# Block results stored by token instead of by block in a two-layer metaformer on one core

## The chip, the cores and the metric

The kernel runs on one core of a Trainium2 chip. The metric is the device time of one execution in microseconds (us), as the median over runs; a profiled execution gives the trace from which durations are read. The core has five engines with a queue each: TensorE (PE, with its weight loads PEld), VectorE (DVE), ScalarE (ACT), GpSimd (POOL) and SyncE (SP). Each runs its own queue in order, and they wait for each other by semaphores. DMAs are issued from SP, ACT and POOL; those with an index per row ("indirect") are issued from POOL here.

## The reference

Everything is float32. x has four images of 384 channels and 32 x 32 tokens. Two layers follow each other, each a mixer and a feed-forward part, with residuals:

```python
x = x + _L0_conv_ref(_ln_c(x), ...)      # attention, 8 heads of 48, relative positions in q, k and v, then proj
t = _to_tokens(x)
t = t + _L0_ffn_ref(_ln_t(t), ...)       # weights are Kronecker products, gelu between
x = _from_tokens(t, x)
x = x + _L1_conv_ref(_ln_c(x), ...)      # sum of depthwise convolutions, at most 7x7
t = _to_tokens(x)
t = t + _L1_ffn_ref(_ln_t(t), ...)       # 4 experts 384 -> 1536 -> 384, each token gated to its best two
x = _from_tokens(t, x)
```

`_ln_c` and `_ln_t` normalise each token over its 384 channels. The expert part takes a softmax over four scores, keeps the two largest, divides them by their sum, and adds the two experts' results with these weights.

## The kernel before

P is 128, C is 384, KC = 3 chunks of channels, N = 1024 tokens an image, B = 4 images, BLK = 128. Sizes in DMA rows are rows of C float32, 1536 bytes. The kernel has three phases.

**qkv_phase** (0 to about 237 us). Eight tiles of 512 tokens. `load(t)` brings a tile of x, three loads bring `wq` (384 x 1152). `token_stats` transposes a tile with `ident` (L75), takes mean and variance on DVE (L77, L78) and 1/deviation (L84, L85); `to_partitions` turns it into a row for all partitions (s_dg L103, all_ps L105). `center` subtracts from each column of the weights its mean, by matmuls with `one` (L116) and DVE (L118), once, ahead of the tiles. Then come six q and k products (qk_ps L163, qk_sb L167, stored to qk_d by POOL) and four v products (v_ps L174), which ACT writes into `va`, 64 wide per head of which 48 are filled; the other 16 have to be zero. `va` is cleared as a whole by POOL at the start (L135), ahead of `ident`'s second step on POOL. From tile 2 to 5 POOL also writes zeros over the whole of `xs_d` (L190, eight DMAs of 3 MB), the padding of the dispatched rows.

**attention_phase** (to about 1663 us) is not touched.

**rest_phase** (to the end). Per image: `front` (proj L903/L906 and the Kronecker feed-forward, L921 to L952), `normalise`, `image` (a padded picture `img`), `convolve`, gates, dispatch. `convolve` runs 49 taps on DVE, one instruction per chunk of channels and tap (L993, 128 x 1024). For image 0 DVE does chunk 0 and the first `own` = 4 rows of chunk 1; the other rows of chunk 1 and chunk 2 are done on PE at the same time by `taps_by_matmul`: four parts (two of 16 rows, two of 14), 196 matmuls each with diagonal weights (L1037), sums by L1047/L1048, added into the image on DVE (L1051). Three steps of this generator are taken per tap of DVE.

`gates` yields for each token its two experts (`mask`) and weights (`gate`), and the normalised token rows. `scatter` computes for each token a slot in its experts' lists (`slot_positions`; `rank` is the place in the list) and POOL writes the rows to `xs_d` by index (L1103), 16 writes of 128 rows an image; `block_list` then makes the list of blocks. A *block* is 128 slots of one expert: 67 blocks in four groups of COUNTS = 13, 16, 16 and 22; the groups follow the images as they are dispatched. For block k, POOL fetches the rows `xg` (L1147) one block ahead and the weights `w` in two halves by index (L1166), three halves ahead; PE transposes xg (xT_ps L1160); then come twelve steps of a first product (e_ps L1198), Gelu on ACT (L1201) and a second product (y_ps L1176), two steps later. DVE adds the bias (yo L1179) and SP stores 128 rows to `y_d`, in the order of blocks (L1181).

`combine(bs)` turns results into the output. `result_rows` computes on DVE, from `rank` and the group's `pieces` (where each expert's list begins in `y_d`), the two rows of `y_d` that belong to each token; POOL gathers them by index (L1237, 16 of 128 rows an image); ACT and DVE weigh and add (L1249, L1250), PE transposes (L1226), DVE adds the residual (L1227), SP stores (L1228). Images 0 to 2 are combined from block `NOT_LAST` = 6 of the last group on, beside the blocks; image 3 after the last block.

**Order.** A scheduler orders each engine's queue by the order of the program's steps and by when operands are free; instructions passed to `keep_in_program_order` stay as written. The program's order is made by generators: within the blocks `more` keeps a small budget of DVE and PE time, and takes steps from `todo` (= `others`: front, normalise and convolve of images 1 to 3) while it is not spent. Inside `others`, each tap of image b also advances `side`, the dispatch of image b-1, by one step (from the third tap on), and `later`, the front of image b+1 (from the thirteenth). `first` is image 0's convolution.

Of the kernel before, what the change touches and what calls it, by code (L numbers as in the profile page):

```python
# [11 lines left out]
F32 = mybir.dt.float32  # L12
AF = mybir.ActivationFunctionType
ALU = mybir.AluOpType
# [4 lines left out]
P = 128  # L19
# [28 lines left out]
CAP = B * N  # L48

# [16 lines left out]
def token_stats(nc, pools, ident, x, eps, rows=None, step=4):  # L66
# [5 lines left out]
    for j in range(nj):  # L72
# [6 lines left out]
        if rows is not None:  # L79
            nc.scalar.copy(rows[j], ps[:, :C])  # L80
# [40 lines left out]
def qkv_phase(tc, cst, x, w_qkv, qk_d, v_d, xs_d):  # L121
# [6 lines left out]
    with ExitStack() as es:  # L128
# [6 lines left out]
        nc.gpsimd.memset(va, 0.0)  # L135
        zero = wp.tile([P, 1, C], F32, name="zero")
# [10 lines left out]
        for k in range(KC):  # L147
            nc.sync.dma_start(wq[:, k, :], w_qkv[k * P : (k + 1) * P, :])
        stats = result(token_stats(nc, (work, psum, "st"), ident, xts[0], cst["eps6"]))
        center(nc, psum, "st", one, wq)  # L150
        for t in range(NT // TOK):
# [8 lines left out]
            for m in range(2 * KC):  # L160
                ps = psmm.tile([P, TOK], F32, tag="mm", name="qk_ps")
# [7 lines left out]
            if t + 1 < NT // TOK:  # L169
                stats = result(token_stats(nc, (work, psum, "st"), ident, xts[t + 1], cst["eps6"]))  # L170
            for j in range(TOK // P):
# [511 lines left out]
def slot_positions(nc, pools, cst, image, count, total):  # L683


    small, psum = pools
# [12 lines left out]
    rank, pos = image["rank"], new(shape, "pos")  # L699
# [15 lines left out]
    for i, pick in enumerate(chosen(nc, new, mask)):  # L715
        for src, dst in ((pos, fpos), (top, image["gate"])):
            nc.vector.tensor_tensor(prod, pick, src, ALU.mult)
            nc.vector.tensor_reduce(dst[:, :, i : i + 1], prod, AX.X, ALU.add)
    nc.vector.tensor_copy(image["pos"], fpos)
# [14 lines left out]


def result_rows(nc, small, image, pieces):


    shape = list(image["mask"].shape)

    def new(shape, name):
        return small.tile(shape, F32, tag=f"p_{name}", name=f"p_{name}", bufs=1)

    pos, part, step = new(shape, "pos"), new(shape, "prod"), new([P, 1, NEXP], "step")
    nc.vector.tensor_tensor(pos, image["rank"], bcast(pieces[0][1].unsqueeze(1), 1, shape[1]), ALU.add)
    for (_, off0), (lo, off) in zip(pieces, pieces[1:]):
        nc.vector.tensor_tensor(step[:, 0, :], off, off0, ALU.subtract)
        nc.vector.tensor_tensor(part, image["rank"], bcast(lo.unsqueeze(1), 1, shape[1]), ALU.is_ge)
        nc.vector.tensor_tensor(part, part, bcast(step, 1, shape[1]), ALU.mult)
        nc.vector.tensor_tensor(pos, pos, part, ALU.add)  # L750
    row = new([P, shape[1], 2], "fpos")
    for i, pick in enumerate(chosen(nc, new, image["mask"])):
        nc.vector.tensor_tensor(part, pick, pos, ALU.mult)
        nc.vector.tensor_reduce(row[:, :, i : i + 1], part, AX.X, ALU.add)
    nc.vector.tensor_copy(image["pos"], row)


def block_list(nc, small, cst, group, parts, done):
# [24 lines left out]
    for i, (lo, _, falling) in enumerate(parts):  # L783
        turn = slice(None, None, -1) if falling else slice(None)
        begin, off = group["pieces"][i]
        nc.vector.tensor_scalar(begin, lo, float(BLK), None, ALU.mult)
        nc.vector.tensor_scalar(
            off, first[:, i * NEXP : (i + 1) * NEXP, 0][:, turn], float(group["start"]), float(BLK), ALU.add, ALU.mult
        )
        nc.vector.tensor_tensor(off, off, begin, ALU.subtract)  # L790
# [20 lines left out]
    nc.vector.scalar_tensor_tensor(where, over, OUTSIDE, where, ALU.mult, ALU.add)  # L811
    nc.vector.tensor_scalar(where, where, slot[:, 0:1], cst["wrow"][:, 0:1], ALU.add, ALU.add)
# [22 lines left out]
def rest_phase(tc, cst, x, ao_d, ins, xs_d, y_d, x2_d, out):  # L835
# [9 lines left out]
    with ExitStack() as es:  # L845
# [31 lines left out]
        pc = {"before": const("before", [P, P]), "blocks": const("blocks", [P, MAXB]), "wrow": const("wrow", [P, 2])}  # L877
        pc["one"], pc["slot0"] = one, const("slot0", [P, NEXP])
# [105 lines left out]
        def convolve(b, xb, parts):  # L984
# [5 lines left out]
            for dy in range(7):  # L990
                for dx in range(7):
                    for k, y0, y1 in parts:
                        nc.vector.scalar_tensor_tensor(  # L993
                            acc[:, k, y0:y1], img[:, k, dy + y0 : dy + y1, dx : dx + IMG],
                            w7[:, k, dy, dx : dx + 1], acc[:, k, y0:y1], ALU.mult, ALU.add,
                        )

# [15 lines left out]
        def taps_by_matmul(xb, parts):  # L1013
# [15 lines left out]
            for k, y0, ny in parts:  # L1029
# [21 lines left out]
                nc.vector.tensor_tensor(acc, acc, po[:, :n], ALU.add)  # L1051
# [8 lines left out]
        for b, nb in enumerate(COUNTS):  # L1060
# [3 lines left out]
                "rank": new([P, nj, NEXP], f"rank{b}"),  # L1064
# [6 lines left out]
                "pieces": [  # L1071
                    (new([P, NEXP], f"begin{b}{i}"), new([P, NEXP], f"off{b}{i}")) for i in range(1 + (b + 1 == B))
                ],
# [8 lines left out]
        scattered = []  # L1082

        def gates(b):
# [9 lines left out]
            for j, row in enumerate(rows):  # L1094
                nc.scalar.activation(row, row, AF.Identity, bias=shift[:, j, :], scale=rstd[:, j, :])
                im["rows"].append(row)
            yield 0.0, 0.0

        def new_row():
            return hid.tile([P, C], F32, tag="rows", name="rows", bufs=16)  # L1100
# [20 lines left out]
        def scatter(b, pause):  # L1121
            im, g = images[b], groups[b]
            slot_positions(nc, (small, ps_m), pc, im, counts[b], counts[b + 1])
            yield 4.0, 0.5
            for j, rows in enumerate(im["rows"]):
                for s in range(2):
# [14 lines left out]
        def blocks(g, more):  # L1141
# [3 lines left out]
            def fetch(k):  # L1145
                xg = ld.tile([P, C], F32, tag="xg", name="xg")
# [8 lines left out]
            def turn(k):  # L1155
# [6 lines left out]
                xT[k] = t  # L1162
# [11 lines left out]
            def second(k, ff, hs, w, py):  # L1174
                o = WB + ff % FH * C
                nc.tensor.matmul(py, hs, w[:, o : o + C], start=(ff == 0), stop=(ff == NF - 1))  # L1176
                if ff == NF - 1:
                    yo = hid.tile([P, C], F32, tag="yo", name="yo", bufs=2)
                    nc.vector.tensor_tensor(yo, py, w[:, WB + FH * C :], ALU.add)  # L1179
                    n = (g["start"] + k) * BLK  # L1180
                    nc.sync.dma_start(y_d[n : n + BLK, :], yo)  # L1181
# [292 lines left out]
```

## Time and profile before

| | |
|---|---|
| median of 3 runs | 3289.18 us (3285.77 to 3293.74) |
| profiled execution | 3284.5 us, of which the span is 3282.7 |
| mean granted clock of TensorE | 0.968 of full speed |
| busy: PE, DVE, ACT, POOL | 91%, 61%, 41%, 35% of the span |
| DMA | 500.60 MB, mean 152 GB/s |

Every time within the execution counts from the start of the span. A row of the timeline has start, duration, engine, line, operation, what is written <- what is read, and in brackets how long the engine was idle before it and what ended that. Busy time is not progress: an engine that waits for nothing and is not on the chain of work that ended last can be slow at no cost. The durations come from the one profiled execution.

### The profile page before, as it was taken

The page shows a single profiled execution, that of the slowest core. Times are in us where ns is not written, and L with a number is a line of the kernel's source. Part 1 is how long each engine was busy: PE and PEld are TensorE (multiplying, and loading weights), DVE is VectorE, ACT ScalarE, POOL GpSimd, SP SyncE. Part 2 cuts the span into 40 slices and gives each one's busy share as a digit, 9 for nine tenths or more (in the row PEclk, how much of TensorE's full clock was granted, in tenths as well). Part 3 has the DMA queues.
Part 4 walks back from the last instruction along what each step waited for, and adds up shares of the span by engine and source line. Part 5 has one row for each costly group of instructions (what it writes and reads, how often), then busy time and mean ns, then how long its engine had stood idle before and what let it go on. Part 6 is the DMA issues. An engine that isn't in the chain of part 4 may idle for free.

```text
span 3282.7 us, 64040 instructions
## 1 busy us (share of the span) xinstructions
PE 2986.8 (91%) x25591; PEld 2063.8 (63%) x25591; DVE 1991.4 (61%) x3619; ACT 1331.7 (41%) x2687; POOL 1159.6 (35%) x1100
## 2 busy tenths in 40 slices
PE   8998998989898989999879888998999999999996
PEld 4445666666675656666643445575577777777775
DVE  2227777768676877777748659998999730001101
ACT  1115656555555655565511131342443333233322
POOL 2225536263536364544520032123125231114422
PEclk9999999999999999999989998998999999999998
DMA  3786464545455555646240313261156035474852
GB/s 140 268 300 195 102 194 115 179 122 174 117 174 129 169 136 141 171 120 187 74 153 23 113 66 142 80 257 56 44 209 234 27 115 213 152 277 151 303 208 70
DMA packets 222202, 500.60 MB, mean 152 GB/s; under 512 B 92192, under 2 KB 145056, under 8 KB 214224
## 3 DMA queue, kind: packets, MB, share of 16 engines
q1 hardware_dynamic: 156720, 214.75, 21.4%
q0 software_dynamic: 43552, 228.24, 18.8%
q10 hardware_dynamic: 21632, 53.52, 6.4%
q8 instruction: 202, 3.31, 0.4%
q14 instruction: 96, 0.79, 0.1%
HBM read 543.58 MB, written 152.37 MB: 212 GB/s over the span
## 4 chain that ended last, share of the span: by engine, by line
PE 65%; DVE 12%; issue 8%; ACT 7%; DMA 5%; POOL 3%; SPq 1%; another core or an unknown queue 0%; ACTq 0%; POOLq 0%; DVEq 0%
PE e_ps L1198 14%; PE y_ps L1176 13%; DVE xb L993 7%; PE av_ps L215 6%; PE t_ps L406 6%; PE tabq_ps L215 5%; PE sc_ps L215 4%; PE tv_ps L215 3%; ACT arow L387 3%; PE tabk_ps L215 2%; PE qk_ps L163 2%; ACT aT L407 2%; PE a_ps L416 2%; DVE oT L470 2%; DMA qs<-qk_d 1%
## 5 line engine op out<-in xcount | busy, mean ns | idle before, releaser
L349 POOL TENSOR_TENSOR bias<-b,s 128x416 f32<-128x416 f32 (+24 forms) x656 | 660.0, 1043 | 631.8 <-DMA s<-sd 424.5
L1198 PEld LDWEIGHTS e_ps<-xT,w 128*128 128x128 f32 x4824 | 654.6, 192 | 230.5 <-issue 16.7
L1198 PE MATMUL e_ps<-xT,w 128*128 128x128 f32 x4824 | 672.6, 277 | 20.2 <-DVE xb L906 8.0
L1176 PE MATMUL y_ps<-w,eh 128*128 128x384 f32 x1608 | 652.5, 490 | 17.7 <-ACT eh L1201 14.3
L993 DVE SCALAR_TENSOR_TENSOR xb<-img,c_w,xb 128x1024 f32<-128x1024 f32 (+1 forms) x539 | 611.0, 1196 | 0.0
L1201 ACT ACTIVATE eh<-e_ps,w 128x128 f32<-128x128 f32 x804 | 293.3, 367 | 753.8 <-PE e_ps L1198 692.3
L1166 POOL DMA_INDIRECT w<-in_w,row x134 | 164.0, 1224 | 786.4 <-PE y_ps L1176 270.7
L377 DVE CUSTOM_DVE_ANT_0 arow<-sc_ps,bias 128x1024 f32<-128x1024 f32 x256 | 312.8, 1222 | 191.4 <-POOL bias L349 101.9
L398 DVE TENSOR_REDUCE extra<-arow 128x32 f32<-128x32 f32 (+24 forms) x768 | 378.7, 551 | 30.2 <-ACT arow L387 30.2
L406 PEld LDWEIGHTS t_ps<-ident,arow 128*128 128x128 f32 x2048 | 226.4, 144 | 265.0 <-ACT arow L387 185.3
L407 ACT COPY aT<-t_ps 128x512 f32<-128x512 f32 x512 | 275.5, 589 | 267.4 <-PE t_ps L406 241.9
L387 ACT ACTIVATE arow<-arow,nm 128x1024 f32<-128x1024 f32 x256 | 297.0, 1160 | 177.6 <-DVE nm L377 166.5
L406 PE MATMUL t_ps<-ident,arow 128*128 128x128 f32 x2048 | 289.1, 286 | 74.4 <-ACT arow L387 73.3
L215 PE MATMUL sc_ps<-kk,qs 48*32 48x512 f32 x4096 | 294.0, 625 | 50.8 <-DMA qs<-qk_d 26.8
L1179 DVE TENSOR_TENSOR yo<-y_ps,w 128x384 f32<-128x384 f32 x67 | 37.2, 556 | 446.9 <-PE y_ps L1176 439.7
L1176 PEld LDWEIGHTS y_ps<-w,eh 128*128 128x128 f32 x1608 | 248.0, 193 | 31.1 <-ACT eh L1201 16.9
L215 PEld LDWEIGHTS av_ps<-aT,vb 128*64 128x64 f32 x4096 | 222.3, 137 | 52.3 <-ACT aT L407 37.8
L303 DVE STREAM_TRANSPOSE b<-tabk_ps 128x480 f32<-128x480 f32 x256 | 219.1, 1000 | 44.5 <-PE tabk_ps L215 24.8
L215 PE MATMUL av_ps<-aT,vb 128*64 128x128 f32 x4096 | 237.7, 274 | 0.0
L215 PE MATMUL tabk_ps<-tab,kq 48*128 48x480 f32 x512 | 225.7, 588 | 3.3 <-DVE b L303 3.3
L215 PE MATMUL tabq_ps<-tab,kq 48*128 48x480 f32 x512 | 224.5, 585 | 0.7 <-ACT va L177 0.7
L308 ACT COPY st<-tabq_ps 128x480 f32<-128x480 f32 x256 | 141.8, 561 | 75.3 <-PE tabk_ps L215 36.5
(212 smaller groups left out, 3190.4 us busy)
## 6 DMA issues: line engine op xcount, KB each, us to landing
sd<-st SPq DMA_DIRECT2D x128, 480.0 KB
s<-sd SPq DMA_DIRECT2D x512, 120.0 KB
xs_d<-zero POOLq DMA_DIRECT2D x8, 3072.0 KB
tvw<-in_tv ACTq DMA_DIRECT2D x120, 192.0 KB
y_d<-yo SPq DMA_DIRECT2D x67, 192.0 KB
qk_d<-qk_sb POOLq DMA_DIRECT2D x48, 256.0 KB
qs<-qk_d SPq DMA_DIRECT2D x256, 48.0 KB
kq<-qk_d ACTq DMA_DIRECT2D x56, 192.0 KB
```

The source lines that it names most:

```text
L215: ins = nc.tensor.matmul(*args, **kw)
L303: turn = nc.vector.transpose(b2.rearrange("p e y x -> p x (e y)")[:, i + j], ps[:, j, : SPAN * IMG])
L349: nc.gpsimd.tensor_tensor(bias[:, y0:y1, :], bass.AP(b2.tensor, b2.offset + (e * IMG + y0) * IMG, [list(b2.ap[0]), [(step * IMG + 1) * IMG ...
L377: nc.vector.tensor_tensor_reduce(s["flat"], ps.rearrange("p h n -> p (h n)"), s["bias"].rearrange("p y x -> p (y x)"), -SCALE, BIG, ALU.ad ...
L387: nc.scalar.activation(s["flat"], s["flat"], AF.Exp, bias=s["nm"], scale=-1.0, accum_out=dn[:, y % YT : y % YT + 1])
L398: pin(nc.vector.tensor_reduce(ex[:, i, :], a[:, p0:p1, :].rearrange("p y x -> p x y"), AX.X, ALU.add))
L406: pin(nc.tensor.transpose(pt[:, j, :], s["flat"][:, k0 : k0 + P], ident))
L407: pin(nc.scalar.copy(aT[:, 4 * g : 4 * g + 4, s["y"] % YB, :], pt))
L993: nc.vector.scalar_tensor_tensor(acc[:, k, y0:y1], img[:, k, dy + y0 : dy + y1, dx : dx + IMG], w7[:, k, dy, dx : dx + 1], acc[:, k, y0:y1 ...
L1176: nc.tensor.matmul(py, hs, w[:, o : o + C], start=(ff == 0), stop=(ff == NF - 1))
L1198: nc.tensor.matmul(ph, w[:, o : o + P], xT[k][:, c, :], start=(c == 0), stop=(c == KC - 1))
L1201: nc.scalar.activation(hs, ph, AF.Gelu, bias=w[:, o : o + 1])
```

## The change

The results of a block are stored by token. Each dispatched row carries two more numbers, its token's row in the result and the base of its first expert's slots (`ids`), so rows of `xs_d` are CX = 386 wide, 1544 bytes. From them DVE computes per block the rows of `z_d` (two rows a token) to which POOL stores `yo` by index; rows of padding or of a block that belongs to another group get an index out of bounds and are not written. `combine` then needs no positions and no index: it loads rows of `z_d` with plain loads from SP, for image 3 half of them from ACT, each after the stores that are in the program by then; `result_rows`, `pieces` and the gathers go. Combining images 0 to 2 starts when 51 stores are in the program.

In qkv_phase, only the padding columns of `va` are cleared, on DVE; `wq` is loaded in nine parts (q, k, v by chunk), and each of q, k and v is centred where it is first used within tile 0. In image 0's convolution `own` is 10, the steps of `taps_by_matmul` are spread evenly over the taps from the third on, and the taps and the adds L1051 keep the order of the program: 14 taps, add, 12 taps, add, 12, add, 11, add. `side` is advanced twice per tap. On POOL's queue the store of a block stands after the fetch of the next xg and ahead of the next two weight halves.

```diff
-        nc.gpsimd.memset(va, 0.0)
-        zero = wp.tile([P, 1, C], F32, name="zero")
+        nc.vector.memset(va[:, :, :, HD:], 0.0)
+        zero = wp.tile([P, 1, CX], F32, name="zero")
...
-        for k in range(KC):
-            nc.sync.dma_start(wq[:, k, :], w_qkv[k * P : (k + 1) * P, :])
+        for i in range(3):
+            for k in range(KC):
+                own = slice(i * C, (i + 1) * C)
+                nc.sync.dma_start(wq[:, k, own], w_qkv[k * P : (k + 1) * P, own])
         stats = result(token_stats(nc, (work, psum, "st"), ident, xts[0], cst["eps6"]))
-        center(nc, psum, "st", one, wq)
...
             for m in range(2 * KC):
+                if t == 0 and m % KC == 0:
+                    center(nc, psum, "st", one, wq[:, :, m * P : m * P + C])
...
+            if t == 0:
+                center(nc, psum, "st", one, wq[:, :, 2 * C :])
             for j in range(TOK // P):
...
-                        nc.vector.scalar_tensor_tensor(
+                        tap = nc.vector.scalar_tensor_tensor(
...
+                        if b == 0:
+                            tc.keep_in_program_order(tap)
...
-                nc.vector.tensor_tensor(acc, acc, po[:, :n], ALU.add)
+                tc.keep_in_program_order(nc.vector.tensor_tensor(acc, acc, po[:, :n], ALU.add))
...
+            nc.vector.tensor_scalar_add(im["ids"][:, :, 0], pc["token"], 2.0 * b * N)
             yield 4.0, 0.5
             for j, rows in enumerate(im["rows"]):
+                nc.scalar.copy(rows[:, C:], im["ids"][:, j, :])
...
-                xg = ld.tile([P, C], F32, tag="xg", name="xg")
+                xg = ld.tile([P, CX], F32, tag="xg", name="xg")
...
-                xT[k] = t
+                at = small.tile([P, 1], F32, tag="at", name="at")
+                nc.vector.tensor_tensor(at, g["first"][:, k, :], xg[:, C + 1 :], ALU.is_gt)
+                to = small.tile([P, 1], U32, tag="to", name="to", bufs=3)
+                nc.vector.scalar_tensor_tensor(to, at, g["over"][:, k, :], xg[:, C : C + 1], ALU.add, ALU.add)
+                xT[k] = t, to
...
-                    n = (g["start"] + k) * BLK
-                    nc.sync.dma_start(y_d[n : n + BLK, :], yo)
+                    stored.append(nc.gpsimd.indirect_dma_start(
+                        to_z.pop(), bass.IndirectOffsetOnAxis(ap=xT.pop(k)[1], axis=0), yo, None,
+                        bounds_check=2 * NT - 1, oob_is_err=False,
+                    ))
...
+            written = list(stored)
...
-                        index = images[b]["pos"][:, n0 // P + j, i : i + 1]
-                        nc.gpsimd.indirect_dma_start(y, None, y_rows, bass.IndirectOffsetOnAxis(ap=index, axis=0))
+                        r0 = 2 * (b * N + n0 + j * P) + i
+                        queue = nc.scalar if end and i else nc.sync
+                        load = queue.dma_start(y[:, :C], from_z[r0 : r0 + 2 * P - 1 : 2, :])
+                        for other in written:
+                            after(load, other)
...
-            half, own = IMG // 2, 4
+            half, own = IMG // 2, 10
...
-            for _ in convolve(0, xbs[0], [(0, 0, IMG), (1, 0, own)]):
-                for _ in range(3):
+            steps = 4 * 27
+            for t, _ in enumerate(convolve(0, xbs[0], [(0, 0, IMG), (1, 0, own)])):
+                for _ in range(steps if t == 48 else max(0, t - 1) * steps // 48 - max(0, t - 2) * steps // 48):
                     next(taps, None)
...
-                    for start, steps in ((2, side), (12, later)):
+                    for start, steps in ((2, side), (2, side), (12, later)):
...
-            if g is groups[-1] and k == NOT_LAST and "combined" not in g:
+            if len(stored) == groups[-1]["start"] + NOT_LAST and "combined" not in groups[-1]:
                 g["combined"] = combine(range(B - 1))
-            spend(g.get("combined", iter(())))
+            spend(groups[-1].get("combined", iter(())))
```

## The prediction

> **What bounds the kernel now.** I read the page first (busy shares, the chain that ended last), then a table of stages, then the timeline at the places that the change touches. Busy time and chain, from the page:
>
> ```profile
> PE 2986.8 (91%) x25591; PEld 2063.8 (63%) x25591; DVE 1991.4 (61%) x3619; ACT 1331.7 (41%) x2687; POOL 1159.6 (35%) x1100
> PE 65%; DVE 12%; issue 8%; ACT 7%; DMA 5%; POOL 3%; SPq 1%; another core or an unknown queue 0%; ACTq 0%; POOLq 0%; DVEq 0%
> ```
>
> TensorE is the bound, so only its idle time can be won. Stages (window, length, busy time of PE, PEld, DVE, ACT, POOL, granted clock, DMA share, GB/s):
>
> ```profile
> 150.00:240.00 90.00, 81.63 (x222) 40.82 (x221) 20.04 (x40) 11.26 (x21) 19.89 (x30) 0.98 0.89 306
> 240.00:1663.00 1423.00, 1279.37 (x16378) 913.38 (x16377) 1041.45 (x1822) 802.11 (x1471) 701.69 (x692) 0.97 0.52 146
> 1663.00:1950.00 287.00, 244.21 (x1365) 105.15 (x1361) 166.55 (x376) 65.11 (x115) 43.38 (x32) 0.91 0.28 96
> 1950.00:2300.00 350.00, 313.57 (x1646) 214.32 (x1645) 336.55 (x512) 112.65 (x247) 78.63 (x56) 0.94 0.35 129
> 2700.00:3000.00 300.00, 296.70 (x1824) 236.50 (x1823) 13.44 (x24) 91.17 (x242) 66.17 (x67) 1.00 0.53 196
> 3000.00:3222.00 222.00, 215.94 (x1326) 171.26 (x1325) 30.29 (x55) 71.53 (x186) 75.49 (x75) 0.99 0.63 233
> ```
>
> Attention (240 to 1663) is not edited. PE has time to give at the start, in 1663 to 2300 (79 us idle) and after 3222; from 2700 to 3222 it has 9.4 us. DVE is 96% busy in 1950 to 2300, so work added there has a price.
>
> The profiled execution took 3284.5 us: 1.8 more than its span, 4.7 under the median of 3289.18. I subtract from 3284.5 and add 4.7 at the end.
>
> **1. Start.** Timeline (start, duration, engine, line):
>
> ```profile
> 0.89 13.76 POOL L135 MEMSET va<- 128x16384 f32 x1
> 15.02 2.82 PE L75 MATMUL row_ps<-ident,xt 128*128 128x128 f32 x12 [15.02 <-POOL ident masks.py:199]
> 17.64 6.87 PE L116 MATMUL sum_ps<-wq,one 128*128 128x384 f32 x18
> ```
>
> The clearing of `va` on POOL holds back `ident`, and with it the first transposes, to 15.0. A quarter of it on DVE runs beside the loads (by width of POOL's row 3.4 us; DVE has nothing else there). The bound becomes the first tile of x: 4.3 MB are loaded from 1 to 14 us at about 400 GB/s once running (2 to 3 us: 111 GB/s), so its 0.79 MB should be there at about 5.5 (not before 4.6). Of these 9.5 us some are lost: the centring of the weights now covers the statistics less well. Before, s_dg came 7.05 after the first transpose (22.07), with centring's DVE work ahead of it; now it should come about 5 after, and PE has 2.8 of transposes for these 5: 2.2 idle. The thirds of centring that come later wait for sum_ps and DVE: another 0.5 to 1. Left: 6. The rest of the stage runs at DMA share 0.89 with PE 91% busy, so DMA may swallow part. Bounds 1 to 9; taken 6. The nine weight loads instead of three put six more issues on SP (0.44 to 0.54 each): beside the transfers, at nothing.
>
> **2. Image 0's convolution.** PE and DVE share chunk 1:
>
> ```profile
> 1806.20 19.31 PE L1037 MATMUL tap_ps<-img,w 64*64 64x448 f32 x196
> 1832.91 1.76 PE L1048 MATMUL taps_ps<-taps,half 128*64 128x448 f32 x4 [7.41 <-DVE xb L1051]
> 1834.60 21.34 PE L1037 MATMUL tap_ps<-img,w 64*64 64x448 f32 x196
> 1858.33 0.62 DVE L1051 TENSOR_TENSOR xb<-xb,taps_ps 128x448 f32<-128x448 f32 x1 [22.99 <-PE taps_ps L1048]
> ```
>
> PE waits 7.4 us for an add that stood behind DVE's taps, then DVE waits 23 for PE. Afterwards the last two PE parts are 352 wide: 352/448 x 19.3 = 15.2 each. PE reaches 1806.2 as before, then 15.2 + 1.6 + 15.2 + 1.4: about 1840. DVE: 1.19 spacing for the 1024 wide tap; for the 320 wide one nothing is shown, between 0.275 (128 wide) and 1.19; from both, linearly, 0.47 (bounds 0.35 to 0.55). From 1760.05: 14 pairs of 1.66, add 0.69; 12 pairs to 1803.9; the second sum is ready only at 1806.2 (2.3 stall), add 0.69; 12 pairs, add 0.55; 11 pairs, add 0.55: 1846. So DVE becomes the end, 12.7 before 1858.95. With the bounds on the spacing, 1841 (PE's) to 1850: 9 to 17; taken 12.
>
> **3. Dispatch advanced twice per tap.** Image 1's tokens are scattered by POOL from 2236.86 to 2259.5 (16 of 0.97 to 1.64); group 0's last block ended at 2244.8, so group 1's first rows come late:
>
> ```profile
> 2256.19 1.33 PE L75 MATMUL row_ps<-ident,xb 128*128 128x128 f32 x5 [3.15 <-DVE xb L906]
> 2265.04 0.88 PE L1160 MATMUL xT_ps<-ident,xg 128*128 128x128 f32 x3 [7.52 <-DMA xg<-xs_d,slot]
> ```
>
> Two steps a tap bring this scatter some 16 taps (20 us) forward, so the 7.5 go, and the front work of the next image has blocks to lie beside; then DVE's adds (L906) are late next. PE idles 15.2 us in 2200 to 2300. Bounds 0 to 12; taken 8. Image 3's scatter is not binding: at 2670, 14 blocks of image 2's group are still to run.
>
> **4. Per block.** Gone: the SP store (0.32 issue). Added: on DVE `at` and `to` (128x1; the same width takes 0.154, so 0.31 a block, waiting for xg, which PE's transposes wait for too), on POOL an indirect store of z_d (0.97 + 0.30, for the xs_d rows; L1166's rows say up to 1.5 to 2 beside the taps). On POOL's queue it stands after the next xg and ahead of the two weight loads; these already waited for the same `yo` (L1179) or for y_ps, so they are late by one issue, 1.3 to 2.1 us, and no wait of PE in the list from 1663 on ends on a weight load. DVE: 29 blocks in 1950 to 2600 x 0.31 = 9 us where DVE is full; a third of it on PE's path: cost 3, bounds 0 to 8. The few operations that fill `ids` (three on DVE and eight 128x2 copies on ACT per image) are by the same row some 0.15 each, beside other work: nothing.
>
> The Trainium skill ("SBUF — State Buffer", section "SBUF: two separate sides") speaks against this part: descriptors of POOL's queue are starved while DVE holds the port they share, which it does in its two-port modes. The trace has the slowing: L1166 takes 1.50 us in 1950 to 2600, 1.01 in 2700 to 3222. By the rule's own example (620 ns becoming 3100) the 29 stores would take some 72 us more of POOL, whose rows there add to 169 of 650 us (L1166 87.1, L1103 41.6, L1147 40.4).
>
> **5. Combine of images 0 to 2.** 48 gathers of 0.98 + 0.30 leave POOL; they stood in front of xg (3105.69 to 3110.78 four gathers, then xg). The loads are now SP's, at its 0.3 to 0.4 an issue, each after 51 stores. result_rows leaves DVE, which is idle there. Of 9.4 us PE idle: bounds 0 to 8, taken 5.
>
> **6. Tail.**
>
> ```profile
> 3250.38 0.56 DVE L1179 TENSOR_TENSOR yo<-y_ps,w 128x384 f32<-128x384 f32 x1 [13.89 <-PE y_ps L1176]
> 3253.64 0.97 POOL L1237 DMA_INDIRECT rows<-y_d,pos  x1 [31.68 <-issue]
> 3275.92 0.61 ACT L1249 ACTIVATE rows<-rows,gate 128x384 f32<-128x384 f32 x1 [3.25 <-DMA rows<-y_d,pos]
> ```
>
> Sixteen gathers 1.27 apart take 20 us; from the last landing to the end are 6.8. Afterwards: the indirect store ends on POOL at 3252.2 and lands 2.57 later (the xs_d rows' landing on the chain at 2255.48): 3254.8. Eight loads on each of two queues are issued within 3.5 us; 3.1 MB at 300 to 400 GB/s (the highest slices of the page; the start) take 8 to 10.5: last rows at about 3264.5, end at 3271 to 3273. Bounds 6 to 12; taken 10.
>
> **7. Rows of 1544 bytes.** Padding, scatter and fetch move 0.5% more. The padding fill (25.2 MB) falls into the fullest DMA stretch, 0.89 at 306 GB/s, that is 344 at full share: 73 us, and PE idles there for DMA behind it (DVE waits 55.0 us in all for qk_d stores in 120 to 240). No row of the trace shows this pitch; bytes alone give 0.4 us, taken as 0.
>
> The Trainium skill ("DMA: Bandwidth & Descriptors", "How a descriptor splits into AXI transactions") is against it: a descriptor that does not start on 256 bytes costs extra beats. By its account 1536 aligned bytes are 48 beats, 1544 unaligned ones 49 to 56: an estimate of 2 to 17%, so 1 to 12 us on the fill. The sum by it would be 26 to 37 instead of 38.
>
> **Sum**: 6 + 12 + 8 - 3 + 5 + 10 = 38. 3284.5 - 38 = 3246.5 profiled, 3251 as a median. All best ends: 9 + 17 + 12 - 0 + 8 + 12 = 58, 3231. All worst: 1 + 9 + 0 - 8 + 0 + 6 = 8, 3281.
>
> **Rivals.**
> - *The middle absorbs*: DVE is full from 1950 to 2600, and what image 0 ends earlier is spent waiting for DVE; 1 and 6 alone carry. For it: PE's waits on L906, L952, L77 add to 24 us in 1863 to 2300. Against: at 2670 PE still has 14 blocks in hand. 16 us: 3273.
> - *More than summed*: with scatters early at every hand-over, PE's idle time at 2000 to 2050 (15.4 us) and 2600 to 2700 (9.7) goes too, half of it 12: 3239 or less.
> - *Slower: the 1544-byte rows halve the fill's rate.* Place: 120 to 230. Price: up to 73 us, 3324. It decides where a row costs over 38/73 = 52% more than before. Against: the bytes grow by 0.5% only, and at a share of 0.89 a tenth of the stretch is free.
>
> **Chances.** Forecast (within 12 us) 0.53; middle absorbs 0.24; more 0.10; no difference 0.04; slower 0.09, most of it the rows. The measurement tells 0.2%, 6.6 us, from no change: faster (under 3282.6) 0.87, same 0.04, slower 0.09. The range is that of the bounds, 3231 to 3281.
>
> **What would show it.** First transposes at about 5.5; last add of image 0's convolution 12 us earlier against its first tap, with PE waiting little; no PE wait on xg at the hand-over from group 0 to 1; one z_d store a block on POOL, and no PE wait on w; last yo to end of span 21 us instead of 32. Wrong if the padding fill holds DMA longer than before, if PE waits for w or for `at`, or if image 1's first block starts no earlier.

## The result, and the profile after

The forecast 38 us were not gained; the changed kernel is as fast as the one before or a little slower: 3295.36 us median (3292.77 to 3297.6, four runs) against 3287.47 for the kernel before in the same runs, ratio 1.0025 with a 95% interval of 1.0001 to 1.0049. A second measurement, on another chip, gave 1.0012 (0.9999 to 1.0025). The profiled execution has a span of 3294.9 us at a mean clock of 0.963.

The kernel before took 3260 us on the chips of three sets of runs and 3288 on those of the other two; every ratio below is to the kernel before on the same chip, and profiles are compared by distances between two instructions. The largest differences between the chips are named at the end.

Busy times and the stages that were shown of before, now of the changed kernel (same columns):

```profile
PE 2988.6 (91%) x25591; PEld 2070.7 (63%) x25591; DVE 2011.9 (61%) x3647; ACT 1334.3 (40%) x2719; POOL 1158.3 (35%) x1102
1663.00:1950.00 287.00, 238.19 (x1414) 106.23 (x1410) 179.34 (x387) 65.73 (x123) 43.28 (x32) 0.90 0.27 95
1950.00:2300.00 350.00, 313.40 (x1671) 218.02 (x1671) 328.37 (x519) 111.56 (x257) 100.44 (x70) 0.94 0.35 130
3000.00:3222.00 222.00, 204.37 (x1244) 162.98 (x1243) 34.92 (x82) 67.73 (x176) 49.55 (x48) 0.96 0.64 229
```

TensorE does the same work in the same busy time (2988.6 against 2986.8), so the question is where its idle time lies. The third stage is where it shows: 3000 to 3222 was well covered in the kernel before, with 6 us idle at a clock of 0.99, and now has 17.6 us idle at 0.96.

Cut at instructions that both kernels have, with two profiled executions of each (us; yo n is the bias add of block n):

| stretch | before | changed | difference | forecast |
|---|---|---|---|---|
| start to first sc_ps | 274.5, 274.3 | 273.8, 274.2 | -0.4 | -6 |
| to first proj of the last phase | 1395.6, 1395.8 | 1397.9, 1396.1 | +1.3 | 0 |
| to first tap matmul | 82.3, 83.2 | 88.2, 88.2 | +5.4 | 0 |
| image 0's convolution, to gate_ps | 105.8, 105.9 | 91.4, 92.2 | -14.1 | -12 |
| to yo 0 | 118.0, 123.1 | 125.8, 121.8 | +3.3 | |
| yo 0 to yo 36 | 770.6, 775.2 | 779.0, 780.3 | +6.8 | -5 for these three |
| yo 36 to yo 51 | 245.8, 246.8 | 243.0, 243.0 | -3.3 | |
| yo 51 to yo 66 (combine beside blocks) | 257.7, 257.3 | 271.2, 270.9 | +13.6 | -5 |
| yo 66 to the end | 32.3, 32.2 | 24.6, 24.1 | -7.9 | -10 |

The differences add to 4.7 (4.5 before rounding). Attention, which no edit touches, took 1391.9 to 1404.7 us in the 17 profiles of this case, so the ends of single profiled executions are not compared below. Now the rows that answer to those of the prediction. The start, and image 0's convolution (timeline of the changed kernel; start, duration, engine, line):

```profile
5.52 2.79 PE L76 MATMUL row_ps<-ident,xt 128*128 128x128 f32 x12 [5.52 <-DMA xt<-in_x]
...
1829.18 15.24 PE L1024 MATMUL tap_ps<-img,w 64*64 64x352 f32 x196
1851.23 5.33 PE L609 MATMUL gate_ps<-xb,c_gate_w 128*32 128x512 f32 x12 [4.78 <-DVE xb L978]
1851.56 0.51 DVE L1038 TENSOR_TENSOR xb<-xb,taps_ps 128x352 f32<-128x352 f32 x1
```

The transposes begin at 5.5 as forecast, and a part of 352 takes 15.2 as forecast. VectorE is now the end of the convolution, and TensorE waits 4.8 us for its last taps. The twelve gate matmuls after that wait take 5.33 us: the clock record shows half speed from 1850 to 1857. In the kernel before they came without a wait:

```profile
1858.22 2.77 PE L602 MATMUL gate_ps<-xb,c_gate_w 128*32 128x512 f32 x12
```

The tail (timeline):

```profile
3270.29 0.56 DVE L1174 TENSOR_TENSOR yo<-y_ps,w 128x384 f32<-128x384 f32 x1 [13.89 <-PE y_ps L1171]
3271.13 1.01 POOL L1175 DMA_INDIRECT z_d<-yo,to  x1 [12.94 <-DVE yo L1174]
3273.69 7.61 SPq L1234 DMA_DIRECT2D rows<-z_d  x8
3281.50 3.85 ACT L1249 ACTIVATE rows<-rows,gate 128x384 f32<-128x384 f32 x7 [4.58 <-DMA rows<-z_d]
```

Sixteen plain loads are issued in 8 us from two queues, and seven of the eight weighings run from 3281.5 on (the first at 3276.3): 24.6 us from the last bias add to the end instead of 32.3. That part held. What went wrong stands in three other places, each an engine's queue that stands behind one held instruction: in two of them behind a wait for a DMA, in one behind work of POOL.

The token numbers, in the last phase before the first tap (timeline, POOL, VectorE and TensorE):

```profile
1689.76 10.85 POOL L1006 TENSOR_TENSOR w<-half,c_w 128x3136 f32<-128x3136 f32 x2 [9.45 <-DVE b_first L769]
1690.41 10.29 DVE L1112 TENSOR_SCALAR ids<-c_token 128x8 f32<-128x8 f32 x4
1701.22 0.90 PE L76 MATMUL row_ps<-ident,xb 128*128 128x128 f32 x3 [9.35 <-DVE s_st L78]
```

The row merges the four images' operations, 128 x 8 each. The second and the fourth take 0.16 us; the first takes 4.82 and the third 5.42. They end at 1695.23 and 1700.63, and the two POOL operations beside them end at 1695.20 and 1700.60: VectorE is held until POOL's operation is over. It is not the constant `token` that it waits for: in pin_weigh below the constant lands at 1695.36 and the first operation starts at 1696.18, and the two take 4.82 and 5.42 us again. The kernel before has one such operation, which ends at 1693.65 beside a POOL operation that ends at 1693.64:

```profile
1688.85 4.80 DVE L775 SCALAR_TENSOR_TENSOR b_slot<-done,c_slot 128x4 f32<-128x4 f32 x1
```

In each of the 17 profiles some VectorE operation ends within 0.03 us after the first of these two POOL operations. Other VectorE operations run beside them at their usual length, such as L891 with 0.74 us at 1691.83 in pin_ids; what makes the difference was not tested. All four images' operations were put there by the scheduler, and they read nothing but a constant. The statistics of image 0 come behind.

The combine of images 0 to 2 beside the blocks: who ScalarE waits for, and who TensorE waits for, 2960 to 3240 (total, times, longest), then the worst place in the timeline:

```profile
ACT rows L1249 <- DMA rows<-z_d: 32.6, 13, 9.1
```

```profile
PE y_ps L1171 <- ACT eh L1198: 9.2, 2, 6.2
PE e_ps L1195 <- ACT xT L1151: 8.4, 2, 8.1
```

```profile
3038.57 0.62 ACT L1249 ACTIVATE rows<-rows,gate 128x384 f32<-128x384 f32 x1 [9.14 <-DMA rows<-z_d]
3039.34 0.47 ACT L1151 COPY xT<-xT_ps 128x384 f32<-128x384 f32 x1
3039.86 1.65 PE L1195 MATMUL e_ps<-xT,w 128*128 128x128 f32 x6 [8.08 <-ACT xT L1151]
```

ScalarE waits 9.1 us for a plain load; the copy of xT stands behind it in its queue, and TensorE behind that. In the kernel before the 24 weighings of images 0 to 2 were spread from 2985.7 to 3150.1, as their gathers took their turn on POOL's queue between the blocks' own fetches. With the loads on SP the scheduler drew them together into 2997.9 to 3071.1. That it was POOL's queue which had kept them apart is read from these times; no run tests it.

### The profile page after: what moved, and what is told of

It reads as the page before. It is cut to its first block, busy times and chain, and to the rows that moved or that the text cites. A ratio compares the mean times of both kernels' runs of the same rounds, so it can differ in the third digit from the quotient of the medians.

```text
span 3294.9 us, 64237 instructions
## 1 busy us (share of the span) xinstructions
PE 2988.6 (91%) x25591; PEld 2070.7 (63%) x25591; DVE 2011.9 (61%) x3647; ACT 1334.3 (40%) x2719; POOL 1158.3 (35%) x1102
## 4 chain that ended last, share of the span: by engine, by line
PE 46%; DVE 12%; issue 6%; DMA 4%; ACT 4%; POOL 1%; ACTq 0%; SPq 0%; another core or an unknown queue 0%; DVEq 0%; POOLq 0%
PE e_ps L1195 12%; PE y_ps L1171 11%; DVE xb L978 8%; PE av_ps L222 4%; PE t_ps L413 3%; PE tabq_ps L222 3%; PE sc_ps L222 2%; PE tv_ps L222 2%; ACT arow L394 2%; PE tap_ps L1024 1%; ACT aT L414 1%; DMA rows<-z_d 1%; PE a_ps L423 1%; DVE oT L477 1%; PE proj_ps L888 1%
## 5 line engine op out<-in xcount | busy, mean ns | idle before, releaser
L978 DVE SCALAR_TENSOR_TENSOR xb<-img,c_w,xb 128x1024 f32<-128x1024 f32 (+1 forms) x539 | 621.4, 1209 | 0.0
L1175 POOL DMA_INDIRECT z_d<-yo,to x67 | 85.4, 1275 | 554.0 <-DVE yo L1174 380.7
```

Of the source, the lines that this page charges most:

```text
L978: tap = nc.vector.scalar_tensor_tensor(acc[:, k, y0:y1], img[:, k, dy + y0 : dy + y1, dx : dx + IMG], w7[:, k, dy, dx : dx + 1], acc[:, k, ...
```

## The experiments

**Weighing kept in order.**

```diff
-                    nc.scalar.activation(z, z, AF.Copy, scale=gate[:, 0:1])
+                    scaled = nc.scalar.activation(z, z, AF.Copy, scale=gate[:, 0:1])
+                    if not end:
+                        tc.keep_in_program_order(scaled)
```

> The changed kernel with one edit: ScalarE's weighing of the rows of images 0 to 2 (L1249) is kept in the order of the program, one item of 256 tokens per ten steps of the blocks, where the scheduler had drawn all twelve items into some 35 steps. Theory A: in the changed kernel these instructions stand in ScalarE's queue ahead of Gelu and of the copy of xT and wait there for plain loads that share the DMA engines with the weights; then the waits of TensorE on ScalarE from 2960 to the last block (8.1, 6.2 and 3.0 us the longest) go, the 16 blocks from number 50 to 66 take 277 us instead of 288, and the kernel gains 9 to 14 us, to some 3283. Rival B: the loads disturb the weight transfers wherever the weighing stands; then the waits move to the weights or to xg and the gain is under 3 us.

Measured: 0.9995 of before (0.9987 to 1.0004). yo 50 to yo 66 takes 264.2 us instead of 287.7. The waits of ScalarE in 2960 to 3240 are now only these, and no wait of TensorE is left in that window:

```profile
ACT eh L1198 <- PE e_ps L1195: 175.4, 183, 1.6
ACT xT L1151 <- PE xT_ps L1150: 8.4, 13, 1.0
ACT eh L1198 <- ACT eh L1198: 0.9, 1, 0.9
```

Theory A held, with a larger effect than it gave: yo 51 to yo 66 is 247.7, some 23 us under the changed kernel (270.4 in pin_ids below, on the same chip, which lacks this edit) and 5 to 10 under the kernel before (257.5; 252.6 on this kind of chip). With the weighing in order the loads hold up no one in this window. The forecast's gain of 5 was in the change, and was lost more than four times over by the order on one queue.

**Token numbers kept in order.**

```diff
-            nc.vector.tensor_scalar_add(im["ids"][:, :, 0], pc["token"], 2.0 * b * N)
+            tc.keep_in_program_order(
+                nc.vector.tensor_scalar_add(im["ids"][:, :, 0], pc["token"], 2.0 * b * N)
+            )
```

> The changed kernel with one edit: the operation on VectorE that fills the token numbers is kept in the order of the program, where the scheduler had put all four of them at the start of the last phase, behind nothing but the load of the constant token. Theory A: VectorE stands 10 us in that wait (1690.4 to 1700.7) with the statistics of image 0 behind it, so the first tap matmul, 88.2 us after the first proj matmul, comes 82 to 83 after it, as before the change, and some 6 us are gained there; at the end of the kernel 3 to 6 of them are left. Rival B: the statistics wait for another constant that lands just as late; then the distance stays at 86 or more.

Measured: the first tap matmul comes 79.6 us after the first proj, against 88.2 in the changed kernel and 87.8 in pin_weigh on the same chip: the gain of theory A, and 3 us more than it gave. The edit works by another way than theory A says: VectorE now loses 3.13 us at b_slot (from 1694.17 to 1697.30, with POOL's operation ending at 1697.28), where the kernel before loses 4.80 and the changed kernel 10.2. The ratio is 1.0057 (1.0038 to 1.0076), on a chip where the changed kernel itself was not run, so it doesn't say what is left of this at the end. Its profile shows a third wait, on VectorE and TensorE after the dispatch of image 0:

```profile
1899.35 0.16 DVE L1156 TENSOR_TENSOR at<-first,xg 128x1 f32<-128x1 f32 x1 [20.12 <-DMA xg<-xs_d,slot]
```

```profile
1902.39 3.78 PE L919 MATMUL f_ps<-u,c_c_fc 32*128 32x512 f32 x12 [7.20 <-DVE u L908]
```

VectorE stands 20 us at the first block's `at`, which needs the first fetched rows; the u product (L908) of image 1's feed-forward stands behind it, and TensorE waits 7.2 us for that and then runs twelve matmuls in 3.78 us that take 1.99 in pins3 below, after a wait of 1.24.

**at and to kept in order.**

```diff
-                nc.vector.tensor_tensor(at, g["first"][:, k, :], xg[:, C + 1 :], ALU.is_gt)
+                tc.keep_in_program_order(nc.vector.tensor_tensor(at, g["first"][:, k, :], xg[:, C + 1 :], ALU.is_gt))
...
-                nc.vector.scalar_tensor_tensor(to, at, g["over"][:, k, :], xg[:, C : C + 1], ALU.add, ALU.add)
+                tc.keep_in_program_order(
+                    nc.vector.scalar_tensor_tensor(to, at, g["over"][:, k, :], xg[:, C : C + 1], ALU.add, ALU.add)
+                )
```

> The changed kernel with one edit: the two small operations of a block on VectorE (at and to) are kept in the order of the program. Theory A: in the changed kernel the first of them stands in VectorE's queue between the two u products (L908) of the feed-forward of image 1 and waits there for the first xg; TensorE's f_ps then waits 7 us and works at half clock after it. Kept behind, the wait of f_ps goes, the first result of the first block comes 60 us after the last write of scatter 0 instead of 70 to 71, and the kernel gains 8 to 12 us. Rival B: the wait stands in for another (the first xg is needed by TensorE too); then the distance stays over 68 and the gain is under 3.

> The kernel before, unchanged, for a profile beside the runs of this set. Theory A: the stall of 7 us on matmuls of the feed-forward of image 1 (1900 to 1910 in the first profile, with no wait on another engine of the core) is a matter of that one execution and is gone here, so that the first block's first result comes 60 us after the last write of scatter 0 instead of 71.6. Rival B: it belongs to the kernel and stands here too, 70 to 72.

> The changed kernel, unchanged, for its ratio beside its edits. Theory A: its stalls (VectorE behind the token constant, 6 us; VectorE behind xg ahead of the feed-forward of image 1, 11; ScalarE behind the plain loads, 20) all belong to the kernel and stand here again, so it is 20 to 30 us slower than the kernel before on this chip, more than the 8 us of the first measurement. Rival B: the ratio of the first measurement holds, 1.0025, 8 us.

These ran on one chip, of the 3288 us kind. The changed kernel came to 1.0012 (0.9999 to 1.0025), nearer to rival B than to theory A. The edit came to 1.0015 (1.0003 to 1.0027): no gain. From the last write of scatter 0 to yo 0 it has 75.4 us; the kernel before has 76.7 in its second profile (71.6 in its first), so there too the stall stayed. On this chip the feed-forward of image 1 stalls by 3.6 to 9.3 us during the scatter or just behind it in every kernel, with a releaser that the profile does not name; in the edited kernel:

```profile
1903.54 0.60 ACT L929 ACTIVATE hs<-f_ps 128x512 f32<-128x512 f32 x1 [6.50 <-remote]
```

On the chips of the 3260 us kind this stall is missing: 59.7 us in conv_alone, 70.5 in pin_ids, and 60.0 in pins3 below, which has this edit. There the wait for `at` costs 10 us; on this chip it lies beside another stall and costs nothing. What that stall is was not settled.

**All three orders, and the fill of xs_d.** Two tiles earlier (fixes), where the change has it (pins3), and one DMA per tile (pins3_spread). The edit of the fill in fixes:

```diff
-            if 2 <= t < 2 + NEXP:
-                rows = xs_d[(t - 2) * CAP : (t - 1) * CAP].rearrange("(n p) c -> p n c", p=P)
+            if t < NEXP:
+                rows = xs_d[t * CAP : (t + 1) * CAP].rearrange("(n p) c -> p n c", p=P)
```

> The changed kernel with the three orders kept (token numbers, at and to, weighing of images 0 to 2) and the fill of xs_d two tiles earlier (tiles 0 to 3 instead of 2 to 5, where the DMA engines are at 0.4). Theory A: each stall goes by itself, 6 + 11 + 18, and the start's 5 us reach the attention because the DMA engines are free again at its beginning: 30 to 45 us faster than the changed kernel, 10 to 25 faster than the kernel before. Rival B: the waits hide each other, or the earlier fill only moves the full stretch to the loads of x; under 20 us faster than the changed kernel, no faster than before.

> The changed kernel with the three orders kept (token numbers, at and to, weighing of images 0 to 2) and the fill of xs_d where the change has it (tiles 2 to 5). Theory A: the kernel with the earlier fill lost 6 to 8 us at the start (the first sc_ps at 280.6 against 274.2), since the stores of qk_d stand behind two fills of 3 MB in the same queue and TensorE then waits in tiles 3 to 6; so this one is 5 to 8 us faster than that: ratio 0.990 to 0.993, the first sc_ps at 273 to 275. Rival B: what was lost at the start came back in attention; same ratio as with the earlier fill, 0.994.

> The same with the fill of xs_d cut into one DMA of 3 MB per tile, tiles 0 to 7, where the change writes two per tile in tiles 2 to 5. Theory A: the 5 us that the new start still has at tile 2 to 5 are lost because two fills in a row hold the qk_d stores for 14 us or more; with one fill (9 us) the buffers cover it, no wait of DVE on qk_d stores over 6 us is left, the last v_ps ends at 228 to 231 instead of 234.5 and the first sc_ps comes at 266 to 270. Rival B: the last fills now collide with the first loads of attention; the last v_ps ends earlier but the first sc_ps comes at 273 or later.

Measured: 0.9942 (0.9923 to 0.9960), 0.9947 (0.9933 to 0.9960) and 0.9965 (0.9951 to 0.9979). On one chip the three orders and the moved fill take the changed kernel from 4 us behind the kernel before (1.0012) to 19 ahead. The place of the fill gains nothing. Two tiles earlier, the last v_ps ends 6 us later than in the changed kernel, from this wait of VectorE in 20 to 250 us (58.8 in the changed kernel):

```profile
DVE qk_sb L172 <- DMA qk_d<-qk_sb: 64.4, 12, 16.9
```

The stores of qk_d stand in POOL's queue behind fills of 3 MB. Spread, the last v_ps ends at 230.1, 5.6 earlier than in pins3 on the same chip, and the first sc_ps comes at 280.8, 4.0 later. That is rival B: the last fill is issued at 232.1 and lands at 252.7, and from 240 to 250 the DMA share is 1.02 and TensorE does nothing. The expectation on pins3 missed: its ratio is that of fixes.

**Two dispatch steps or one.** side_alone is the kernel before with only this edit; pins3_side1 takes it back from pins3.

```diff
-                    for start, steps in ((2, side), (12, later)):
+                    for start, steps in ((2, side), (2, side), (12, later)):
```

> The three orders kept, and the dispatch advanced once per tap as before the change. It tells what two steps are worth. Theory A: two steps bring the scatter only some 7 to 11 us forward while the front of the next image, which covered TensorE's wait for the first rows, has moved behind it (proj of image 3 at 2271 instead of 2245; wait on xg 13.1 us instead of 7.5 + 3.2 + 2.4), so they are worth nothing or cost: with one step this kernel is as fast or up to 5 us faster than the one with two, and yo 0 to yo 36 takes 770 to 774 us instead of 779 to 781. Rival B: two steps gain the 8 us of the forecast, and this kernel is 5 to 10 us slower.

> The kernel before with the dispatch advanced twice per tap and nothing else. Theory A: scatter 1 comes 7 to 11 us earlier, but the front of image 3 moves behind it, TensorE waits 10 to 13 us for the first rows of group 1 instead of 7.5, and yo 0 to yo 36 takes 5 to 10 us more; ratio 1.001 to 1.003. Rival B: the waits only change places; ratio 0.9990 to 1.0010. Rival C: the 8 us of the forecast are gained; ratio under 0.9985.

Measured: side_alone 1.0017 (1.0007 to 1.0027), with 770.4 us from yo 0 to yo 36 where five profiles of other edits of the kernel before on this kind of chip have 765.4 to 767.6 (conv_alone and the new start's four). pins3_side1 0.9934 (0.9921 to 0.9947), 768.4 us against 778.6 in pins3. So two steps cost about 5 us by themselves and 10 us in this stretch beside the three orders. The hand-over to group 1 with one step (conv_alone):

```profile
2234.08 0.89 PE L75 MATMUL row_ps<-ident,xb 128*128 128x128 f32 x5 [3.13 <-DVE xb L906]
2242.95 0.87 PE L1162 MATMUL xT_ps<-ident,xg 128*128 128x128 f32 x3 [7.99 <-DMA xg<-xs_d,slot]
```

and with two (side_alone):

```profile
2254.31 0.88 PE L1160 MATMUL xT_ps<-ident,xg 128*128 128x128 f32 x3 [10.77 <-DMA xg<-xs_d,slot]
```

The scatter of image 1 starts 250 us after yo 0 instead of 262 and ends 3.9 us after yo 12 instead of 14.2. But the proj work of image 3, which lay in that gap, now comes after it, and TensorE waits 10.8 us with nothing beside it: yo 12 to yo 20 takes 221.1 us against 221.4. So nothing is won at the hand-over; the 5 us are lost in small pieces before and after it (1.5 from yo 0 to yo 12, 3.2 from yo 20 to yo 36). One piece is a wait of TensorE for a block's weights near 2500, 3.0 us in side_alone and 3.5 in pins3, which the two kernels with one step do not have; the rest was not settled. pins3_side1 is the fastest kernel measured here: 3240.24 us against 3262.01 for the kernel before, a gain of 22 us. The forecast without its parts 1 and 3, which brought little or nothing here, is 12 - 3 + 5 + 10 = 24.

**Parts alone on the kernel before**: the start, image 0's convolution, and the start with rows of 1544 bytes (the two more numbers are filled and not used). The edits are those of the change's diff.

> The kernel before with image 0's convolution alone changed (ten rows on VectorE, steps spread, order kept). Theory A: from the first tap matmul to the last add 92 us instead of 106.6, a gain of 14; but the front of image 1, dispatch of image 0 and the slow clock after the wait of 4.8 us before the gates take back about half: the first e_ps 6 to 9 us earlier against the first tap, and the kernel gains 4 to 9. Rival B: what follows holds the first block to a fixed time (its stall near 1902 to 1910 ended at the same time in both kernels though one came 4 us earlier); then the kernel gains under 3. Rival C: all 14 are carried to the end, 12 or more.

Measured: 0.9969 (0.9958 to 0.9980), 10 us; 92.7 us from the first tap to gate_ps instead of 105.8. Between theories A and C: 13 are won in the convolution and 10 of them are carried to the end.

> The kernel before with the start alone changed (padding of va cleared on VectorE, weights of qkv in nine loads, centring by thirds). Theory A: the 9 us gained at the first transposes are taken back by the fill of xs_d, which keeps the DMA engines full until 246 us, so that the stage of attention begins when it did: the last v_ps 2 us earlier, the first sc_ps within 1 us of before, and the whole kernel within 3 us of before. Rival B: the gain is lost only later, by chance of the clock; then the first sc_ps is 6 or more earlier and the kernel gains 4 to 9.

> The kernel before with the new start, and rows of 1544 bytes in xs_d (the two more numbers are not used; everything else as before). With rows of 1536 the new start alone had its first sc_ps at 268.3 and the first proj at 1662.8, 6 to 7 earlier than before. Theory A: the wider rows take these away: the fill of 25.2 MB takes 1.5% longer per packet and, with the stores behind it, moves the first sc_ps to 272 or later. Rival B: the rows cost only their 1 us, and the first sc_ps stays at 267 to 270; then the loss in the changed kernel comes from something else in its start.

> The kernel before with the new start alone, a second execution. Theory A: the 3 us at the first qk_ps (14.8 in its first execution, 16.4 to 17.8 in all others with the new start) were chance; now the first qk_ps stands at 16.4 to 17.8, the last v_ps ends at 232 to 235 and the first sc_ps at 271 to 274. Rival B: rows of 1536 bytes are what makes the start 6 us earlier; then 14.8, 230 and 268 again.

> The same with rows of 1544 bytes, a second execution. Theory A: within 2 us of the other at the last v_ps and the first sc_ps. Rival B: 4 or more later than it at both.

Measured: 0.9990 (0.9981 to 0.9999) and 0.9993 (0.9984 to 1.0002). The first sc_ps of the new start comes at 268.3 and 272.5; on the same two chips conv_alone and side_alone, whose start is that of the kernel before, have 272.6 and 274.5. So the new start brings attention forward by 4.4 and 2.0 us in the two executions, and the ratio says 3 us (0.3 to 6). With rows of 1544 the first sc_ps comes at 274.1 and 273.7. The second stands on the chip of the 272.5, so the wider rows cost 1.2 there; on the chip of the 268.3, pin_weigh and pin_ids, which have the new start and the wider rows, come at 272.7 and 274.4, which is 4 to 6 later. What the wider rows cost at attention's begin is not settled by these. Step by step, in the second execution of the new start against side_alone: -9.5 at the transposes, -6.6 at the first qk_ps, -2.9 at tile 2, -4.9 at the last v_ps, -2.0 at the first sc_ps.

## Why the prediction was wrong, point by point

- **Part 5 is the step that failed most**: +13.6 instead of -5. It priced what leaves POOL and what SP issues, and did not ask what had kept the weighings apart. The gathers seem to have, as in POOL's queue they could not pass the blocks' fetches. That the order of the weighings cost the time is shown by pin_weigh (247.7 against 270.4 us on one chip); that the gathers had kept them apart is read from the times.
- **Part 4's "nothing" for `ids`** cost 5.4. The price of 0.15 each was that of an operation which nothing disturbs; two of the four took 4.82 and 5.42 us, until POOL's operations beside them ended, and image 0's statistics stood behind them in VectorE's queue. The kernel before lost 4.80 us in this way at one operation, and its trace had the row. That their place in the queue cost the time is shown by pin_ids; that POOL holds them is read from the ends of the operations, which agree in every profile.
- **Part 4's `at`** was said to wait for what TensorE waits for too. But TensorE comes to it after the feed-forward of image 1, and VectorE stood in front of that feed-forward. 10 us on one kind of chip, hidden on the other. The rest of part 4 was right: with the three orders kept and one dispatch step, yo 0 to yo 36 is 768.4 us, 1 to 3 over the edits of the kernel before; the forecast had 3. The 67 z_d stores take 1.28 us each in the mean.
- **Part 3** has the wrong sign: -8 forecast, +5 measured in side_alone. The scatter did start earlier. What "is late next" was put on VectorE's adds; it was the first rows again, since the cover had gone with the step.
- **Part 1** was right at 5.5 and, with a loss of 4.5 of the 9.5 by tile 2 (45.6 instead of 50.6), nearly right there; the rest is given back in the fill and at attention's first wait. The bounds of 1 to 9 did not go down to no gain; 0.4 came. On the kernel before the same start brought 2.0 and 4.4, inside the bounds.
- **Parts 2 and 6** held: -14.1 for -12, -7.9 for -10.
- **Part 7** held: in the trace's records of single DMA packets, a packet of three rows of the fill takes 204 ns instead of 201, 1.5%, 1 us over the fill. The estimate from "How a descriptor splits into AXI transactions" in the Trainium skill's "DMA: Bandwidth & Descriptors" was 2 to 17%; the trace is below its lower end. The estimate was worked out for single rows and the packets hold three, so this is no test of the page's account. What the wider rows cost beyond the packets, at attention's begin, stays open. The rival that was slower, by these rows, is refuted; that nothing was gained came by a way that no rival had.

The sum of the misses is 18.6 (part 5) + 5.4 (ids) + 11.8 (parts 3 and 4 between gate_ps and yo 51) + 5.6 (start) + 1.3 (attention) + 2.1 (tail) - 2.1 (convolution) = 42.7, which is the 38 that were forecast and the 4.7 that came instead.

## What to carry to other kernels

When an operation is moved off a queue, ask what that queue's order had held back: with nothing to hold them, a scheduler may place the loads' consumers early, and every engine queue that they stand in waits with them. Price a small new operation by what can hold it (a load, or another engine's work beside it) and by what is queued behind it, not by its duration, and read this in the new order of instructions before pricing anything else. A step that makes something earlier must also be asked what it takes the cover from.

## What was not expected of the hardware

- TensorE's half clock after a wait makes the wait cost more than its length: after 8.08 us without work six matmuls took 1.65 us where the rows around have 0.83, after 4.78 us twelve took 5.33 instead of 2.77, after 7.20 twelve took 3.78 instead of 1.99 (the first two in the changed kernel, whose record has half speed from 3034.6 to 3044.9 and from 1850.2 to 1857.0; the third in pin_ids, with half speed from 1900.1 to 1913.7). Over the whole execution no difference shows: the record has 245 and 231 us at half speed in the two profiles of the changed kernel, 210 and 231 in those of the kernel before.
- A small VectorE operation can take as long as a POOL operation beside it: operations on 128 x 8 and 128 x 4 elements took 1.8 to 5.4 us instead of 0.12 to 0.16, and ended 0.02 to 0.03 us after POOL's operation of 5.44 us.
- The kernel before takes 3260 us on some chips and 3288 on others at nearly the same granted clock (0.967 to 0.972 in edits of it on the one kind, 0.965 and 0.968 on the other). Stage by stage the profiles differ while POOL scatters image 0 (106 us from gate_ps to yo 0 against 118 to 123), between yo 0 and yo 36 (765 to 768 against 771 to 775), between yo 36 and yo 51 (242.5 against 246), and in 5 us of the combine (252.6 against 257.5). A hidden stall on one chip is an open one on another: `at` cost 10 us on the one kind and nothing on the other.
